# A quantised feed-forward at the end of a two-layer decoder: transposes by DMA, the down projection one tile behind, and a written order for five engines

## The chip, the cores and the metric

The program runs on one core of a Trainium2 chip. A core has a matrix engine (TensorE, here PE, with its weight loads PEld), a vector engine (VectorE, DVE), an activation engine (ScalarE, ACT), a general engine (GpSimd, POOL) and a queue engine that issues DMAs (SyncE, SP). The engines run side by side, each through its own instructions in a fixed order, and wait for each other by semaphores. The metric is the device time of one execution in microseconds (us), as the median over runs.

## The reference, cut to what matters

The model is a decoder of two layers on four batches of 512 rows with 512 features. Each layer has self-attention, cross-attention and a feed-forward, and a layernorm follows every one. The change concerns the last of the six blocks, the second layer's feed-forward, whose weights are rounded to -1, 0 or 1 and whose rows are rounded to 8 bits:

```python
def _quant_act(x):
    s = jnp.max(jnp.abs(x), axis=-1, keepdims=True) / 127.0 + EPS
    xq = jnp.clip(jnp.round(x / s), -128.0, 127.0)
    return (xq, s)

def _qlinear(x, w):
    wq, ws = _quant_weight(w)
    xq, xs = _quant_act(x)
    y = jnp.einsum('bsi,oi->bso', xq, wq)
    return y * xs * ws

gate = jax.nn.silu(_qlinear(x, w_gate))
up = _qlinear(x, w_up)
return _qlinear(gate * up, w_down)
...
x = _layernorm(x + _L1_ffn_ref(x, L1_ffn_w_gate, L1_ffn_w_up, L1_ffn_w_down), axis=-1)
```

Gate and up go from 512 to 2048 features, down goes back to 512. A row's scale needs its largest absolute value, so the down projection of a row can begin only when all of its 2048 hidden values are there.

## The kernel before, in words

All 2048 rows stay in SBUF as 16 tiles `X[t]` of 128 rows by 512 features in float32. The blocks follow one another; the weights of the last feed-forward are loaded, scaled and rounded to bfloat16 during the block before it, the cross-attention (`quantized`).

That cross-attention (`l1_xattn`, its loop in `run`) runs under a manual schedule: a loop over steps writes down the order of the instructions on PE, DVE and ACT by hand. Each step computes scores twice (`first_pass`, L1214, for the row maxima of L1218; `second_pass`, L1230, for the exponentials of L1234), and other work is hung on certain steps with `plan(step, place, function)`. POOL and SP aren't in that schedule; a scheduler orders their instructions. The last batch's output projection (L1287, added in at L1292) ends the block.

The feed-forward (`l1_ffn`, L1419 to L1482) has no written order: the scheduler arranges all engines. It goes over the 16 tiles with `pipelined`, which calls `first` for tile t+1 before `second` for tile t.

`first(t)` rounds the rows (`quantize`: maximum L1426, scale L1427 and L1429, division on DVE L1430, narrowing to bfloat16 on ACT L1431). The rounding is done by adding and subtracting the large constant `ROUND`. A matmul needs its left operand with the features along the partitions, so `flipped` turns the tile: four PE transposes of 128x128 (L1437) into PSUM and one DVE copy out of it (L1438). For each of four parts of 512 hidden features, PE then sums four matmuls for gate (`ps_s`) and four for up (`ps_m`); these go through the helper `mm`, so they carry line L160. ACT applies silu with the row's scale (L1455), DVE multiplies by up and its scale (L1456).

`second(t)` takes the largest absolute value of the 2048 hidden values (L1462, L1463), the scale (L1464, L1465), divides (four of L1468 on DVE), narrows (four of L1469 on ACT), turns 16 blocks on PE with four copies on DVE (L1437, L1438), sums 16 down matmuls in `ps_m` (L160), and adds the scaled sum to `X[t]` (L1476). After the fourth tile of a batch, `layernorm` computes moments (L219, L220), a square root on ACT (L243, with a table load, since silu's table is another), a reciprocal (L244), four norms on DVE (L239), and stores the four tiles (L1480).

PSUM has three banks for `ps_s`, two for `ps_t`, three for `ps_m` in this block.

Of the kernel before, what the change touches and what calls it, by code (L numbers as in the profile page):

```python
# [10 lines left out]
BF16 = mybir.dt.bfloat16  # L11
# [6 lines left out]
P = 128  # L18
B, S, F = 4, 512, 512
T = B * S  # L20
# [66 lines left out]
def decoder_kernel(ctx: ExitStack, tc: tile.TileContext, a: dict, out: bass.AP):  # L87
# [134 lines left out]
    def inverse_roots(b):  # L222


        mv, y = moments[b]
        v, t = small(4, "var"), small(4, "newton")
        G.tensor_scalar(v, mv.rearrange("p (t s) -> p t s", s=2)[:, :, 1], LN_EPS, None, ALU.add)
# [8 lines left out]
    def normalise_tile(b, i):  # L236
        mv, rstd = moments[b]
        x = X[4 * b + i]
        V.tensor_scalar(x, x, mv[:, 2 * i:2 * i + 1], rstd[:, i:i + 1], ALU.subtract, ALU.mult)  # L239

    def table_roots(b):
        mv, rstd = moments[b]
        A.activation(rstd, mv.rearrange("p (t s) -> p t s", s=2)[:, :, 1], AF.Sqrt, bias=LN_EPS)  # L243
        V.reciprocal(rstd, rstd)  # L244
# [864 lines left out]


# [6 lines left out]
    def l1_xattn():  # L1117
# [189 lines left out]
        for M in range(4 * B):  # L1307
# [40 lines left out]
            for i in range(4):  # L1348
                plan(t0 + norms[i], LATE, normalise_tile, b, i)
        for name, n, steps in (("L1_ffn_gateT", INNER, (2, 17, 19)), ("L1_ffn_upT", INNER, (35, 53, 54)),  # L1350
                               ("L1_ffn_downT", F, (68, 85, 110))):
            quantized(plan, name, n, *steps)
# [66 lines left out]
    def l1_ffn():  # L1419
# [4 lines left out]
        def quantize(x, scratch, xq, s):  # L1424

            V.tensor_reduce(s, x, AX.X, ALU.max, apply_absolute_value=True)  # L1426
            V.tensor_scalar(s, s, 1.0 / 127.0, Q_EPS, ALU.mult, ALU.add)  # L1427
            inv = small(1, "one", 8)
            V.reciprocal(inv, s)  # L1429
            V.tensor_scalar(scratch, x, inv, ROUND, ALU.mult, ALU.add)  # L1430
            A.activation(xq, scratch, AF.Copy, bias=-ROUND)  # L1431

        def flipped(dst, src, n):
            for c in range(n // 4):
                pt = pst(BF16)
                for i in range(4):
                    PE.transpose(pt[:, tk(i)], src[:, tk(4 * c + i)], identb)  # L1437
                V.tensor_copy(dst[:, 4 * c:4 * c + 4, :], pt.rearrange("p (k n) -> p k n", k=4))  # L1438

        def first(t):  # L1440
            s = small(1, "one", 8)
            xq, xqt = tmp(BF16), prob("q", [4, P], 3, BF16)
            quantize(X[t], tmp(), xq, s)
            flipped(xqt, xq, 4)
            gs, us = small(1, "one", 8), small(1, "one", 8)
            V.tensor_tensor(gs, s, sg, ALU.mult)
            V.tensor_tensor(us, s, su, ALU.mult)
            h = [prob("P", [512], 8) for _ in range(4)]
            for n in range(4):
                pg, pu = pss(), psm()  # L1450
                nn = slice(512 * n, 512 * n + 512)
                mm(pg, chunks(xqt), [w[:, nn] for w in wg])
                mm(pu, chunks(xqt), [w[:, nn] for w in wu])
                g = tmp()
                A.activation(g, pg, AF.Silu, scale=gs)  # L1455
                V.scalar_tensor_tensor(h[n], pu, us, g, ALU.mult, ALU.mult)  # L1456
            return h

        def second(t, h):
            part, s, inv = small(4, "part4"), small(1, "one", 8), small(1, "one", 8)  # L1460
            for n in range(4):
                V.tensor_reduce(part[:, n:n + 1], h[n], AX.X, ALU.max, apply_absolute_value=True)  # L1462
            V.tensor_reduce(s, part, AX.X, ALU.max)  # L1463
            V.tensor_scalar(s, s, 1.0 / 127.0, Q_EPS, ALU.mult, ALU.add)  # L1464
            V.reciprocal(inv, s)  # L1465
# [70 lines left out]
```

## Time and profile before

| What | us |
|---|---|
| median of three runs | 2851.83 |
| the three runs | 2848.3 to 2853.07 |
| the profiled execution's own time | 2832.23 |
| its span | 2830.5 |
| first gate matmul of the last feed-forward, from the span's start | 2611.22 |
| last addition of a down sum begins | 2821.31 |

The span is the time from the first to the last recorded instruction of one profiled execution. For each engine the page gives busy time and instructions; a second view gives the same by stage, with the granted PE clock as a share of full speed. Another follows the chain of work that ended last: start, length, engine, tile and line of each piece, each released by the one before it. A line of the timeline has start, length, engine, line, operation, the tile written and those read with their shapes, how often, and in brackets how long the engine had been idle and for whom. A line on DMAs has the tiles, the issuing queue, the number, the size and the median time from issue to landing. PE's matmuls are pipelined and their ends are modelled, so the distance from one group's start to the next is the better measure of them.

### The profile page before, as it was taken

To read this page: it belongs to the slowest core of one execution; us is meant where nothing else is said; L and a number is where in the kernel's file an instruction comes from. 1 tells how busy PE (TensorE), PEld (TensorE's weight loads), DVE (VectorE), ACT (ScalarE), POOL (GpSimd) and SP (SyncE) were. 2 spreads that over 40 slices of the span, in tenths; PEclk is the share of its full clock that TensorE was granted. 3 is DMA by queue.
4 is the path that set the end of the run, shared out by engine and by line. 5 is a ranking of instruction groups with operands and counts; after the bars stand their busy time and mean duration, and the time that the engine had idled before them with its cause. 6 is when DMAs were issued, how large, how long until landed. Compare 5 with 4: busy or idle time off the path is not lost.

```text
span 2830.5 us, 30402 instructions
## 1 busy us (share of the span) xinstructions
PE 2714.3 (96%) x11434; PEld 1329.1 (47%) x11434; DVE 1693.2 (60%) x3551; ACT 1050.4 (37%) x1929; POOL 423.0 (15%) x436
## 2 busy tenths in 40 slices
PE   7999999898989989999999999999999999999897
PEld 3444444474556435555555555553334334334443
DVE  4555554554211467566765665665766766675998
ACT  2333433233222123233323332233565564554443
POOL 3000000024000401001101110124332332211000
PEclk9999999899999999999999999999999999999999
DMA  9700000002330301000000000110112021010000
GB/s 391 294 15 1 15 5 27 23 16 94 127 113 21 129 30 60 0 1 1 1 0 1 1 1 30 45 64 34 60 60 71 27 87 45 12 53 1 16 16 31
DMA packets 61128, 142.76 MB, mean 50 GB/s; under 512 B 6537, under 2 KB 26010, under 8 KB 54818
## 3 DMA queue, kind: packets, MB, share of 16 engines
q1 hardware_dynamic: 54818, 123.80, 12.2%
q0 software_dynamic: 6144, 16.79, 1.7%
q8 instruction: 99, 1.62, 0.2%
q14 instruction: 67, 0.55, 0.1%
HBM read 84.73 MB, written 47.45 MB: 47 GB/s over the span
## 4 chain that ended last, share of the span: by engine, by line
PE 57%; DVE 7%; ACT 1%; issue 1%; POOL 0%; DVEq 0%; ACTq 0%; POOLq 0%
PE ps_m L160 16%; PE ps_b L1230 8%; PE ps_m L934 7%; PE ps_m L979 5%; PE ps_s L947 5%; PE ps_m L1241 4%; PE ps_t L964 2%; PE ps_m L1162 2%; PE ps_b L1214 2%; PE ps_m L1287 2%; DVE P L1456 1%; PE ps_m L1176 1%; PE ps_s L160 1%; DVE P L1468 1%; PE ps_m L1223 1%
## 5 line engine op out<-in xcount | busy, mean ns | idle before, releaser
L1218 DVE TENSOR_REDUCE maxes<-ps_b 128x2 f32<-128x1024 f32 x256 | 312.7, 1223 | 178.3 <-PE ps_b L1214 177.9
L160 PE MATMUL ps_m<-w,attnT 128*128 128x512 f32 (+1 forms) x992 | 382.0, 539 | 0.0
L1234 ACT ACTIVATE PT<-ps_b 128x1024 f32<-128x1024 f32 x256 | 260.9, 1023 | 234.6 <-PE ps_b L1214 152.2
L1214 PE MATMUL ps_b<-k,q 32*128 32x512 f32 x1024 | 286.3, 640 | 1.7 <-ACT PT L1234 1.6
L1230 PE MATMUL ps_b<-q,k 32*128 32x512 f32 x1024 | 283.6, 639 | 0.6 <-ACT PT L1234 0.6
L934 PE MATMUL ps_m<-xT,w 128*128 128x512 f32 x512 | 261.1, 595 | 0.0
L313 DVE TENSOR_TENSOR x<-x,ps_m 128x512 f32<-128x512 f32 x128 | 88.0, 687 | 264.0 <-PE ps_m L160 263.8
L160 PEld LDWEIGHTS ps_m<-w,attnT 128*128 128x128 f32 x736 | 139.0, 191 | 168.6 <-issue 163.8
L951 ACT ACTIVATE P<-ps_s,nmax 128x512 f32<-128x512 f32 (+3 forms) x256 | 135.2, 528 | 182.1 <-DVE nmax L949 179.7
L906 POOL TENSOR_TENSOR q<-tmp 128x512 f32<-128x512 f32 x64 | 81.2, 1269 | 692.6 <-DVE tmp L905 624.3
L947 PE MATMUL ps_s<-k,q 128*128 128x512 f32 (+3 forms) x512 | 180.1, 434 | 0.9 <-ACT P L951 0.9
L370 ACT ACTIVATE P<-ps_s,nmax 128x512 f32<-128x512 f32 x128 | 88.5, 693 | 203.4 <-DVE nmax L368 203.4
L979 PE MATMUL ps_m<-PT,v 128*128 128x512 f32 (+3 forms) x512 | 161.6, 436 | 1.6 <-ACT PT L969 1.6
L969 ACT COPY PT<-ps_t 128x512 f32<-128x512 f32 (+1 forms) x128 | 61.1, 477 | 239.3 <-PE ps_t L964 239.3
L160 PE MATMUL ps_m<-w,xT 128*128 128x512 f32 (+1 forms) x384 | 143.6, 529 | 3.3 <-DVE v L338 3.3
L1230 PEld LDWEIGHTS ps_b<-q,k 32*128 32x128 f32 x1024 | 75.9, 183 | 147.3 <-issue 119.9
L964 PEld LDWEIGHTS ps_t<-kc,P 128*128 128x128 f32 x640 | 83.8, 141 | 120.9 <-issue 79.2
L1241 PE MATMUL ps_m<-PT,vv 128*32 128x512 f32 x1024 | 136.4, 605 | 0.6 <-ACT PT L1234 0.6
L979 PEld LDWEIGHTS ps_m<-PT,v 128*128 128x128 f32 x512 | 92.3, 192 | 94.3 <-issue 50.4
L348 PE MATMUL ps_m<-xT,w 128*128 128x512 f32 x256 | 121.0, 599 | 10.6 <-DMA w<-in_L_attn_Wq 10.6
L949 DVE TENSOR_REDUCE nmax<-ps_s 128x1 f32<-128x512 f32 (+3 forms) x256 | 124.7, 487 | 4.6
L948 DVE TENSOR_TENSOR ps_s<-ps_s,mask 128x128 f32<-128x128 f32 x256 | 73.1, 289 | 80.3 <-PE ps_s L947 80.3
(285 smaller groups left out, 4439.7 us busy)
## 6 DMA issues: line engine op xcount, KB each, us to landing
hidden<-w SPq DMA_DIRECT2D x16, 1024.0 KB, 17.0
result<-w SPq DMA_DIRECT2D x16, 1024.0 KB, 16.9
w<-in_L_ffn_gateT SPq DMA_DIRECT2D x8, 1024.0 KB, 5.0
tmp<-tmp POOLq DMA_DIRECT2D x64, 128.0 KB, 2.0
w<-in_L_ffn_upT SPq DMA_DIRECT2D x8, 1024.0 KB, 4.9
w<-in_L_ffn_downT SPq DMA_DIRECT2D x8, 1024.0 KB, 5.1
w<-in_L_attn_Wqkv SPq DMA_DIRECT2D x6, 1024.0 KB, 7.0
w<-in_L_attn_Wo SPq DMA_DIRECT2D x5, 1024.0 KB, 12.2
```

What stands on the lines that cost most here:

```text
L160: PE.matmul(ps, lhsT=x, rhs=y, start=(i == 0), stop=(i == n - 1))
L934: PE.matmul(ps_q[n], lhsT=wq[h // 4][:, i, tk(h % 4)], rhs=st["xt"][:, i, :], start=(i == 0), stop=(i == 3))
L947: PE.matmul(s[:, :w], lhsT=q[:, tk(qi)], rhs=k[:, :w], start=True, stop=True)
L949: V.tensor_reduce(nmax[:, qi:qi + 1], s[:, :w], AX.X, ALU.max, negate=True)
L951: A.activation(p[:, :w], s[:, :w], AF.Exp, bias=nmax[:, qi:qi + 1], accum_out=sums[:, qi:qi + 1])
L964: PE.transpose(pt[:, tk(qi)], probs[qi][:, tk(c)], ident)
L979: PE.matmul(av[:, c * P:], lhsT=st["v"][:, c, tk(g)], rhs=pts[c][:, c * P:], start=(c == 0), stop=(c == 3))
L1214: PE.matmul(s[:, j, :], lhsT=q[strip(i), tk(qi)], rhs=k[strip(i), :], start=True, stop=True)
L1218: V.tensor_reduce(at[:, 2 * half:2 * half + 2, 16 * (1 - g % 2)], s, AX.X, ALU.max, negate=True)
L1230: PE.matmul(s[:, j, :], lhsT=k[strip(i), tk(c)], rhs=q[strip(i), :], start=True, stop=True)
L1234: A.activation(p, s, AF.Exp)
L1241: PE.matmul(avs[g][strip(i), :], lhsT=vv[c][:, 4 * m + i, 16 * par:16 * par + 32], rhs=pts[g, c, i // 2][:, i % 2, :], start=(c == 0), sto ...
```

## The change

The rows of tiles 0 and 1 are rounded during the cross-attention, in six pieces planned at its steps 113 to 118 (`first_rows`). In the feed-forward, division of the rows and half of the division of the hidden values go to POOL. All turning is done by DMA transposes issued from SP (`dma_start_transpose`): one of 128x512 for a tile's rows, two of 128x1024 for its hidden values, both in bfloat16, straight from SBUF to SBUF; PE's transposes and DVE's copies go. Maxima, divisions and narrowings of the hidden values work on 1024 features at once. The down matmuls of tile k-1 stand behind the gate and up matmuls of tile k (the last three tiles' down matmuls stand at the end). Moments are computed tile by tile; the root of all but the last two tiles is computed on POOL by Newton steps (`inverse_roots`), the norm is applied on ACT by scale and shift for all but the last, and each tile is stored by itself. The whole loop is under a manual schedule for PE, DVE, ACT, POOL and SP, so the order of the lines is the order of the instructions on each. `inverse_roots`, `normalise_tile` and `table_roots` get parameters for one tile.

The diff, cut:

```diff
-    def normalise_tile(b, i):
+    def normalise_tile(b, i, engine=V):
...
+    def scale_of_row(s):
+        inv = small(1, "one", 8)
+        V.tensor_scalar(s, s, 1.0 / 127.0, Q_EPS, ALU.mult, ALU.add)
+        V.reciprocal(inv, s)
+        return inv
+
+    def largest(t):
+        s = small(1, "one", 8)
+        V.tensor_reduce(s, X[t], AX.X, ALU.max, apply_absolute_value=True)
+        rounded[t] = s, scale_of_row(s)
+
+    def divide(t, x):
+        G.tensor_scalar(x, X[t], rounded[t][1], ROUND, ALU.mult, ALU.add)
+
+    def turn_rounded(t, x, xq, xqt):
+        A.activation(xq, x, AF.Copy, bias=-ROUND)
+        nc.sync.dma_start_transpose(xqt, xq)
+        rounded[t] = rounded[t][0], xqt
...
+        for t in range(2):
+            for part in range(3):
+                plan(113 + 3 * t + part, LATE, first_rows, t, part)
...
-        def quantize(x, scratch, xq, s):
-        def flipped(dst, src, n):
-        def first(t):
-        def second(t, h):
-        pipelined(range(T // P), first, second)
...
+        def scales_of(t):
+            scales[t] = small(4, "sums", 3)[:, 0:2]
+            G.tensor_scalar(scales[t], both, rounded[t][0], None, ALU.mult)
+
+        def gate_and_up(t, n):
+            if n == 0:
+                hidden[t] = [prob("h", [2, 512], 4) for _ in range(2)], small(4, "nmax", 3)[:, 0:2]
+            pg, pu, g = pss(), psm(), prob("silu", [512], 3)
+            nn, xs = slice(512 * n, 512 * n + 512), chunks(rounded[t][1])
+            mm(pg, xs, [w[:, nn] for w in wg])
+            mm(pu, xs, [w[:, nn] for w in wu])
+            A.activation(g, pg, AF.Silu, scale=scales[t][:, 0:1])
+            V.scalar_tensor_tensor(hidden[t][0][n // 2][:, n % 2, :], pu, scales[t][:, 1:2], g,
+                                   ALU.mult, ALU.mult)
+
+        def largest_of(t, i):
+            h, part = hidden[t]
+            V.tensor_reduce(part[:, i:i + 1], flat(h[i]), AX.X, ALU.max, apply_absolute_value=True)
+
+        def divide_hidden(t):
+            h, part = hidden[t]
+            s, ds = small(1, "one", 8), small(1, "one", 8)
             V.tensor_reduce(s, part, AX.X, ALU.max)
+            inv = scale_of_row(s)
+            for i, engine in enumerate((V, G if t < N - 1 else V)):
+                engine.tensor_scalar(flat(h[i]), flat(h[i]), inv, ROUND, ALU.mult, ALU.add)
+            G.tensor_tensor(ds, s, sd, ALU.mult)
+            hidden[t] = h, ds
+
+        def turn_hidden(t, i):
+            hq, hqt = prob("hq", [1024], 3, BF16), prob("hqt", [8, P], 6, BF16)
+            A.activation(hq, flat(hidden[t][0][i]), AF.Copy, bias=-ROUND)
+            nc.sync.dma_start_transpose(hqt, hq)
+            turned.setdefault(t, []).extend(chunks(hqt))
+
+        def down(t):
+            ps_d[t] = pst()
+            mm(ps_d[t], turned.pop(t), wd)
+
+        def add_down(t):
+            V.scalar_tensor_tensor(X[t], ps_d.pop(t), hidden.pop(t)[1], X[t], ALU.mult, ALU.add)
+            tile_moments(t // 4, t % 4)
+            (inverse_roots if t < N - 2 else table_roots)(t // 4, slice(t % 4, t % 4 + 1))
+
+        def store(t):
+            mv, rstd = (x[:, t % 4 * n:] for x, n in zip(moments[t // 4], (2, 1)))
+            if t == N - 1:
+                normalise_tile(t // 4, t % 4)
+            else:
+                shift = small(1, "one", 8)
+                G.tensor_scalar(shift, mv[:, 0:1], rstd[:, 0:1], -1.0, ALU.mult, ALU.mult)
+                A.activation(X[t], X[t], AF.Identity, scale=rstd[:, 0:1], bias=shift)
+            nc.sync.dma_start(out[tk(t), :], X[t])
...
+        with tc.manual_schedule(engines={e.engine for e in engines}):
+            for k in range(N):
+                ahead = k + 2 < N
+                if 2 <= k < N - 1:
+                    add_down(k - 2)
+                if k:
+                    turn_hidden(k - 1, 0)
+                gate_and_up(k, 0)
+                if k:
+                    turn_hidden(k - 1, 1)
+                if ahead:
+                    largest(k + 2)
+                gate_and_up(k, 1)
+                largest_of(k, 0)
+                if ahead:
+                    x = prob("x", [512], 2)
+                    scales_of(k + 2)
+                    divide(k + 2, x)
+                gate_and_up(k, 2)
+                gate_and_up(k, 3)
+                if 2 <= k < N - 1:
+                    store(k - 2)
+                if ahead:
+                    turn_rounded(k + 2, x, prob("xq", [512], 2, BF16), prob("xqt", [4, P], 3, BF16))
+                largest_of(k, 1)
+                divide_hidden(k)
+                if 1 <= k < N - 2:
+                    down(k - 1)
+            for i in range(2):
+                turn_hidden(N - 1, i)
+            for t in (N - 3, N - 2, N - 1):
+                down(t)
+                add_down(t)
+                store(t)
```

In the order that results, the first four gate matmuls of tile 0 stand in PE's order ahead of the last attention group's transposes of its sums (L1261). In SP's order the two first row transposes stand ahead of the last load of the down weights.

## The prediction

> **What bounds the kernel now.** I read four views in this order: the busy shares, the busy time by stage, the chain that ended last over one tile, and the end of the timeline.
>
> The first lines of the page (span; then busy time, share and instructions of each engine):
> ```profile
> span 2830.5 us, 30402 instructions
> PE 2714.3 (96%) x11434; PEld 1329.1 (47%) x11434; DVE 1693.2 (60%) x3551; ACT 1050.4 (37%) x1929; POOL 423.0 (15%) x436
> ```
> PE looks saturated, but the share is a mean over all stages, and the change touches only the last 220 us. Busy time by stage, each stretch two tiles long (PE, PEld, DVE, ACT, POOL; then granted clock, DMA share, GB/s):
> ```profile
> 2635.00:2661.00 26.00, 24.11 (x138) 11.71 (x137) 24.52 (x64) 12.34 (x21) 0.00 (x0) 1.00 0.00 1
> 2661.00:2687.00 26.00, 23.80 (x135) 11.51 (x133) 23.43 (x63) 11.58 (x18) 0.00 (x0) 1.00 0.11 41
> 2687.00:2713.00 26.00, 23.19 (x138) 11.49 (x137) 24.46 (x65) 12.71 (x22) 0.00 (x0) 1.00 0.00 1
> ```
> Here DVE is as busy as PE (24.5 of 26 us), ACT half, POOL idle, DMA near idle. The chain over one tile shows what sets the pace:
> ```profile
> 2646.86 1.04 PE ps_s L160 x4
> 2647.89 0.86 PE ps_m L160 x4
> ...
> 2652.32 0.76 DVE P L1456
> 2653.10 0.69 DVE part L1462
> ...
> 2654.10 0.74 DVE P L1456
> 2654.84 0.66 DVE attnT L1438 x2
> 2655.51 0.59 DVE part L1462
> ...
> 2656.93 0.60 DVE one L1426
> 2657.53 1.19 DVE P L1468 x3
> 2658.71 0.66 DVE x L1476
> 2659.37 0.34 DVE q L1438
> 2659.72 0.05 issue
> 2659.76 0.39 PE ps_s L160
> ```
> Next tile's first gate matmul (2659.76) starts 12.90 us after this one's (2646.86). The first half of the chain is matmuls at 0.86 us for four (0.216 each); the second half is DVE work in a row, ending in L1438, the copy out of PSUM of the rounded rows that PE has turned. So the stage is a loop PE to DVE to PE, with DVE's order in it, and not PE alone. Over the stage: first gate matmul 2611.22, last down sum added from 2821.31; 210.1 us for 16 tiles, 13.13 each (the layernorm at the end of a batch costs some).
>
> The end of the timeline:
> ```profile
> 2821.31 0.75 DVE L1476 SCALAR_TENSOR_TENSOR x<-ps_m,one,x 128x512 f32<-128x512 f32 x1 [2.48 <-PE ps_m L160]
> 2823.49 1.92 DVE L239 TENSOR_SCALAR x<-x,mv,rstd 128x512 f32<-128x512 f32 x4
> 2824.07 1.80 SPq L1480 DMA_DIRECT2D out<-x  x4
> ```
> From the last addition to the end of the span 9.2 us: four norms, four stores.
>
> **The change part by part.** *PE.* The 20 transposes a tile go. What stays is 48 matmuls, 48 x 0.216 = 10.37 us. If nothing else delays PE, 16 tiles take 165.9 us instead of 210.1: **-44.2**.
>
> *Can DVE follow?* It loses five PSUM copies (0.416 each), the norm (0.54), half of the hidden rounding and the row rounding (0.48). Left per tile: four products 4 x 0.748 = 2.99; two maxima over 1024, not shown in this form, between 2 x 0.68 x 2 = 2.72 (L1462 twice) and 2 x 1.22 = 2.45 (L1218, from PSUM), I take 2.45 to 2.72; row maximum 0.68; add-down 0.75; moments 0.69 + 0.18; one division over 1024 0.735 (L1090); five small ones at 0.15. Sum 9.2 to 9.5, under 10.37.
>
> *POOL* gets 15 one-column root instructions (4.7 us from 2583.46 to 2589.26 with the 1.04 us of L1091 taken out), three small ones (0.2 each), a division over 512 and one over 1024. L1091 shows 1.04 for 1024 with constants; with a per-row scalar the bounds are 1.04 and, by L906's 1.27 for 512, 2.5. POOL: 6.9 to 9.1, under 10.37 too. I take the low end, same operation class. *ACT*: four silus 0.685, two narrowings of 1024 at 1.05 (L1096), 0.63 for the row (L1431), about 0.62 for the norm: 6.1. Silu, copy and norm share a table in the changed order, so the eight table loads inside the stage (four L243, four L1455, 1.28 each, at batch ends) shrink to three around its start and one in the tail. *SP* gets four issues a tile, 0.39 each by the store row (L1480), in the order hidden half 0, half 1, store, rows.
>
> *The queue that decides: DMA transposes.* Per tile two of 256 KB and one of 128 KB, all in SP's queue. The trace has none. Rows, KB and us from issue to landing:
> ```profile
> tmp<-tmp POOLq DMA_DIRECT2D x64, 128.0 KB, 2.0
> result<-P SPq DMA_DIRECT2D x18, 256.0 KB, 2.2
> w<-turned SPq DMA_DIRECT2D x32, 64.0 KB, 3.9
> bias<-in_b_rows SPq DMA_DIRECT2D x5, 256.0 KB, 8.4
> ```
> Bounds for 256 KB: 2.2 (plain copy) and 8.4. I take 4.0, of which 2.0 hold the queue: the nearest in kind is the 64 KB row that is spread over few partitions (3.9), since a turn, too, breaks rows up. Then a tile's queue is busy 2.0 + 2.0 + 1.0 = 5.0 of 10.37 us.
> On the deadline: in the steady loop hidden(t) is divided about 10.5 us after its tile's first matmul (last matmul 6.9, product 0.75, maximum 1.2, small ones 0.6, division 0.74, handovers). ACT narrows half 0 first thing in the next tile: 11.7, half 1 behind one silu: 13.4. PE wants half 0 at 10.37 + 6.91 = 17.3 and half 1 eight matmuls later, 19.0. So a landing may take 5.5 us before PE waits; 4.0 fits. Behind the two narrowings stand the silus: silu 0 runs at 12.3 instead of 11.4, but PE has three banks for gate and three for up (5.2 us of lead), so PE doesn't feel it.
>
> The Trainium skill speaks both ways here. *VectorE: DVE Perf Modes*, "The three transpose paths", gives the DMA crossbar 1309 ns for 128x128 in bf16 against 390 ns on TensorE; taken one block after another that would be 20 x 1.31 = 26 us a tile, an estimate of some 250 us lost. *DMA: Bandwidth & Descriptors*, "Latency and other measured facts", has 261 GB/s for a DMA transpose; 640 KB a tile would then be 2.5 us, an estimate with no loss. Neither is shown by a run here, and neither is a term of the sum.
>
> *Head.* First rows of tiles 0 and 1 are rounded and turned during the cross-attention, at its steps 113 to 118. DVE's share of it, 2 x (0.68 + 0.30), lies beside a PE that is the bound there (in the last 97 us of that stage DVE waited 19.3 us for score matmuls, PE 4.8 for anything): 0, at most +2. In exchange the four transposes, their copy and PE's 0.72 wait between 2609.9 and 2611.22 go, -1.3, and the first four gate matmuls now stand in PE's order where it waited 0.94 for DVE's sums, **-2.2** in all.
> *Filling the pipe.* In tile 1 no down matmuls lie between: its first silu waits behind tile 0's narrowing, which comes 4.7 us after tile 0's last matmul plus the old batch's four norms (0.42 each at pace); PE runs out of gate banks for about 1.6 us, and down(0) then waits some 2.1 for its turned half: **+3.7**.
> *Tail.* Behind the last up matmul PE has two held-back down groups, 6.9 us. With no down group between tiles 14 and 15 ACT is late as in tile 1: its last silu ends some 2.5 after the last up matmul. Then product 0.75, maximum 1.2, small ones 0.6, division 0.74, narrowing 1.05 and 4.0 of landing: 10.8, less 6.9, so PE stands about **+4.0**. From the last addition on only one tile is normed and stored: three norms of 0.48 less, **-1.6**.
>
> Sum: -44.2 - 2.2 + 3.7 + 4.0 - 1.6 = -40.3, and +0.5 for the mixing in the cross-attention: **-40**. The profiled execution took 2832.23 (span 2830.5) and would take 2792; the runs' median, 2851.83, is 19.6 us higher for a cause the trace doesn't show, so I carry the difference over: **2812**.
>
> **The rivals.** *Late turns, still a gain.* If a 256 KB turn holds the queue 4.6 us, a tile takes 2.5 x 4.6 = 11.5 instead of 10.37: 16 x 1.13 = 18, so 2830. For it: nothing here shows a turn. Against: every 256 KB row that isn't queued behind others is below 3.
> *Orders that catch on each other.* Five engines now have a written order. If DVE works 15% slower beside POOL (9.5 becomes 10.9) with a handover or two, 11.3 a tile: +15, 2827. Against: L1090 takes 0.72 to 0.75 beside POOL's L1091.
> *Slower than before: the turns are the bound.* Place: SP's queue, three turns a tile. It decides from 10.37 + 40/16 = 12.87 us a tile, which is 12.87/2.5 = 5.15 us of queue for 256 KB. At 6 us a tile takes 15.0: 16 x 4.63 = +74, 2812 + 74 = 2886. For it: the 8.4 us row, if it is time of moving and not of queueing. Against: it fell in the start, with DMA busy 97%.
> *No effect:* that the new order leaves DVE the pace-setter at about 13: then near 2850. Against: its sum of 9.5.
>
> **How the numbers follow.** Forecast 0.60 (own range 2803 to 2822: landing 2.3 to 5, and the runs' own spread of some 5 us); late turns 0.16; catching orders 0.08; turns as the bound 0.13; no effect 0.03. Within 0.2% (6 us), what a measurement can hardly tell from no change, lies only the last. Faster 0.84, same 0.03, slower 0.13. The range leaves out the bound turns and the worst of the late ones: 2802 to 2845.
>
> **What will show it.** Right: in the last stage gate matmuls 10.4 us apart, tile to tile; PE's busy time near the stretch; waits of PE only in tile 1 and before the last down group; turns landing within 5.5 us; DVE near 9.5 of 10.4. Wrong: PE waiting for hqt at every down group (turns late), SP's queue without gaps (turns the bound), or gate matmuls waiting for silu (orders catch). The prediction falls if a 256 KB turn holds the queue above 4 us, or if the first 2590 us change by more than 2 us.

## The result: 2815.18 us against 2852.09, and the profile after

The median of four runs of the changed kernel is 2815.18 us (2806.61 to 2818.3), that of the kernel before 2852.09 (2848.3 to 2853.07). The ratio is 0.9868 with a 95% interval of 0.9848 to 0.9888, so 37 us faster. The prediction had 2812, faster. The sum behind it was less good than its result, and most of what follows is about that.

The page of the changed kernel begins as follows (span; then busy time, share and instructions of each engine):
```profile
span 2816.5 us, 29952 instructions
...
PE 2700.2 (96%) x11097; PEld 1313.9 (47%) x11114; DVE 1642.5 (58%) x3313; ACT 1047.2 (37%) x1905; POOL 511.9 (18%) x724
```
The shares say as little as before: 14 us less of PE and 51 us less of DVE don't show what happened. The view by stage does, again with stretches of two tiles (PE, PEld, DVE, ACT, POOL; then granted clock, DMA share, GB/s):
```profile
2651.12:2671.84 20.72, 20.61 (x96) 9.37 (x97) 18.77 (x37) 11.61 (x16) 12.35 (x41) 1.00 0.38 86
2671.84:2692.55 20.71, 20.61 (x95) 9.40 (x96) 17.91 (x33) 11.76 (x16) 11.95 (x41) 1.00 0.41 92
2692.55:2713.30 20.75, 20.64 (x96) 9.43 (x97) 17.95 (x33) 11.76 (x16) 12.00 (x41) 1.00 0.48 90
```
Two tiles take 20.7 us instead of 26 or so, PE is busy in all of it, DVE in 17.9 to 18.8 of it, POOL in 12, and the DMA engines some 40% of it. The chain over one tile has nothing but PE in it:
```profile
2672.00 0.86 PE ps_s L160 x4
2672.86 0.86 PE ps_m L160 x4
...
2678.91 3.45 PE ps_t L160 x16
2682.36 0.86 PE ps_s L160 x4
```
From one tile's first gate matmul to the next it is 10.36 us. The loop from PE to DVE and back, which set the pace before, is gone.

The end of the timeline, and the last drains (an engine's closing instruction at the end of the program, line L1609: how many, duration in ns as minimum, median and maximum, first and last start):
```profile
2799.73 1.46 PE L160 MATMUL ps_t<-w,hqt 128*128 128x512 bf16 x3 [3.09 <-DMA hqt<-hq]
...
2804.86 0.26 POOL L1524 TENSOR_SCALAR one<-mv,rstd 128x1 f32<-128x1 f32 x1 [2.66 <-DVE rstd L244]
2805.14 0.75 DVE L1514 SCALAR_TENSOR_TENSOR x<-ps_t,one,x 128x512 f32<-128x512 f32 x1 [0.38 <-POOL one L1524]
```
```profile
L1609 POOLq DRAIN  x3: 44/113/10873, 2804.8 to 2816.2; - x3
L1609 SPq DRAIN  x3: 7/7/13, 2810.4 to 2815.9; - x3
```
PE stands 3.09 us for the last tile's turned rows. From the last addition (2805.14) to the end of the span it is 11.4 us, where it was 9.2 before and 7.6 were predicted. POOL's drain begins at 2804.8, as POOL's last instruction, the shift of tile 14, comes up, and takes 10.9 us. SP, which has the stores, is done at 2810.4 and waits for it.

**A measure for what follows.** The profiled spans differ by 14 us only (2830.5 and 2816.5), the medians by 37. The stage alone is a firmer measure: from the last matmul of the cross-attention's output projection (its last start is 2609.9 before, 2631.4 after) to the end of the span. It is 2830.5 - 2609.9 = **220.6 us before and 185.1 after**, 35.5 less. (In the changed kernel the four gate matmuls that moved ahead, 0.9 us, lie in front of this mark.) Where the other 20 us lie, before the stage, the third experiment tells. "Stage" below means this measure.

### The profile page after: what moved, and what is told of

Same layout as the page of the kernel before. It is cut to its first block, busy times and chain, and to the rows that moved or that the text cites. A ratio compares the mean times of both kernels' runs of the same rounds, so it can differ in the third digit from the quotient of the medians.

```text
span 2816.5 us, 29952 instructions
## 1 busy us (share of the span) xinstructions
PE 2700.2 (96%) x11097; PEld 1313.9 (47%) x11114; DVE 1642.5 (58%) x3313; ACT 1047.2 (37%) x1905; POOL 511.9 (18%) x724
## 4 chain that ended last, share of the span: by engine, by line
PE 59%; DVE 4%; issue 1%; ACT 1%; another core or an unknown queue 1%; POOL 0%; DVEq 0%; POOLq 0%; ACTq 0%
PE ps_m L160 16%; PE ps_b L1255 8%; PE ps_m L934 7%; PE ps_m L979 5%; PE ps_s L947 5%; PE ps_m L1266 4%; PE ps_t L964 2%; PE ps_m L1187 2%; PE ps_b L1239 2%; PE ps_m L1312 2%; PE ps_s L160 2%; PE ps_t L160 1%; PE ps_m L1201 1%; DVE maxes L1243 1%
## 5 line engine op out<-in xcount | busy, mean ns | idle before, releaser
L160 PE MATMUL ps_m<-w,attnT 128*128 128x512 f32 x736 | 324.0, 598 | 9.8 <-DVE x L313 9.8
L947 PE MATMUL ps_s<-k,q 128*128 128x512 f32 (+3 forms) x512 | 180.1, 434 | 0.8 <-ACT P L951 0.8
L160 PE MATMUL ps_m<-w,xT 128*128 128x512 f32 (+2 forms) x414 | 151.8, 519 | 4.0 <-DVE v L338 3.4
L160 PE MATMUL ps_m<-PT,w 128*128 128x512 f32 (+1 forms) x248 | 115.5, 594 | 7.7 <-PEq L833 3.8
```

What stands on the lines that cost most here:

```text
L160: PE.matmul(ps, lhsT=x, rhs=y, start=(i == 0), stop=(i == n - 1))
L947: PE.matmul(s[:, :w], lhsT=q[:, tk(qi)], rhs=k[:, :w], start=True, stop=True)
```

## The experiments

All ratios are to the kernel before, from runs on the same chip as the experiment's.

**1. The tail without GpSimd.** Tiles 13 to 15 take the root from the table and the norm on DVE, and the last hidden scale is multiplied on DVE.
```diff
-            G.tensor_tensor(ds, s, sd, ALU.mult)
+            (G if t < N - 1 else V).tensor_tensor(ds, s, sd, ALU.mult)
...
-            (inverse_roots if t < N - 2 else table_roots)(t // 4, slice(t % 4, t % 4 + 1))
+            (inverse_roots if t < N - 3 else table_roots)(t // 4, slice(t % 4, t % 4 + 1))
...
-            if t == N - 1:
+            if t >= N - 3:
                 normalise_tile(t // 4, t % 4)
```


> In the tail GpSimd gets nothing: tiles 13 to 15 take their roots from the table and their norm on VectorE, and the last hidden scale is multiplied on VectorE. GpSimd's last instruction is then the scale of tile 14 (2787.1 in the changed kernel's profile) instead of the shift of tile 14 (2804.9). Theory 1 (GpSimd's drain sets the end): its 10.8 us begin near 2787 after the span's start of the changed kernel, end near 2798, and lie beside work; from the last addition to the end of the span 6 to 7 us instead of 11.4, so the kernel gains 4.5 to 5.5 us over the changed one. Theory 2 (the end of a program takes about 8.5 us after the last store is issued, whatever GpSimd did): the drain is still the last thing, the end moves by less than 1 us.

Measured: median 2807.21, ratio 0.9853 (0.9836 to 0.9869), stage 180.1, so 5.0 less than the changed kernel; from the last addition (2793.19) to the end of the span 6.5 us. Its drains:
```profile
L1609 POOLq DRAIN  x3: 44/174/12318, 2773.7 to 2799.4; - x3
L1609 SPq DRAIN  x3: 7/7/13, 2798.4 to 2799.0; - x3
```
POOL's drain now starts at 2773.7, as its last division begins, and is over at 2786, beside PE's work; SP's at 2798.4 is the last. Theory 1 holds: the drain's place, not its being there, cost 5 us.

**2. The changed kernel once more.** No edit.

> The changed kernel once more, for comparison on the same chip. The feed-forward's part (first gate matmul behind the cross-attention to the last addition) repeats the first profile's within 1 us: tiles 10.37 us apart, a wait of about 3.1 us before the last down group, 10.8 us of drain on GpSimd from 2 us before the last addition. Theory 1 on the 20 us that the profile of before lacks against its own runs: the gather of the layer-0 feed-forward (925 to 990 us) is the only stage that differs by more than 2 us between profiles, and differs from execution to execution. Theory 2: it is a property of the changed program (its code lies elsewhere), then it repeats within 2 us in every execution.

Measured: median 2815.83, ratio 0.9879 (0.9862 to 0.9895); span 2816.7, stage 185.0, tiles 10.36 apart, wait before the last down group 3.17, drain of 10,872 ns from 2805.0. The stage repeats within 0.1 us. The first matmul of layer 1's attention starts at 990.6 here and at 990.0 in the first profile, so this run alone would have spoken for theory 2, a property of the program. The other experiments, whose program is the same there, speak against it: they start that attention at 978.7 (experiment 1), the others between 979.9 and 988.0; and the changed kernel's own four runs spread over 11.7 us (2806.61 to 2818.3).

**3. The kernel before once more.** No edit.

> The kernel before, profiled once more. Theory 1 (its first profile caught a lucky gather in the layer-0 feed-forward, which its timed runs did not have): the first matmul of layer 1's attention starts 976 to 992 us after the span's start, not at 970.5, and from there to the end it takes 1859 to 1861 us as before: span 2836 to 2852. Theory 2 (the 20 us between the first profile and the timed runs lie elsewhere, or come with timing as such): the gather's stage repeats within 2 us of 970.5.

Measured: 2853.75, span 2852.0, first matmul of layer 1's attention at 991.0 instead of 970.5; from there to the end 1861.0 us (before: 1860.0), stage 220.6 again. The stretch in front of it is the gather of layer 0's feed-forward. The waits there (window from 900 to 1000; us in total, times, longest; `remote` means that this profile doesn't show who ended the wait), once in this profile of the kernel before, once in the changed kernel's:
```profile
DVE x L313 <- remote: 22.4, 4, 9.1
```
```profile
DVE x L313 <- remote: 15.4, 2, 9.1
```
The first profile of the kernel before has no such line. So one kernel shows both, 970.5 and 991.0; the first profile had caught a short gather. The 19.6 us between it and its runs' median, which the prediction carried over as unexplained, are this. Why the gather takes 0 to 20 us longer in most executions is open.

**4. First rows not planned into the cross-attention.** Rounding and turning of tiles 0 and 1 are written at the head of the feed-forward, outside the manual schedule.
```diff
+        late = rounded.setdefault("late", [])
...
-                plan(113 + 3 * t + part, LATE, first_rows, t, part)
+                late.append((first_rows, t, part))
...
+        for f, t, part in rounded.pop("late"):
+            f(t, part)
         for t in range(2):
             scales_of(t)
```


> The first rows of tiles 0 and 1 are rounded and turned when the feed-forward begins, not during the cross-attention. Theory 1 (the head was a gain of 2.2): PE then stands for a row maximum 0.68, scale 0.3, division 0.7, narrowing 0.6 and a landing of 3.2, in all 5.5 us, less the 2 us by which the layer's last additions are ready ahead of PE's last matmul: 4 to 6 us longer than the changed kernel. Theory 2 (the rows were hidden by other work anyway, or their place in the cross-attention costs what it saves): within 1 us.

Measured: median 2816.14, ratio 0.9888 (0.9868 to 0.9907), stage 185.2, as the changed kernel. But the edit didn't make the rows late: in its trace the first maximum of L1121 starts at 2264.6, where the changed kernel has it at 2553.2. Outside the written order the scheduler moved the rows ahead, as their tile is finished early. The run only shows that this work fits in anywhere; what late rows cost wasn't measured.

**5. Norm and all of the hidden division on DVE again.**
```diff
-            for i, engine in enumerate((V, G if t < N - 1 else V)):
+            for i, engine in enumerate((V, V)):
...
-            if t == N - 1:
+            if True:
                 normalise_tile(t // 4, t % 4)
```


> The second half of the hidden division and the norm go back from GpSimd and ScalarE to VectorE. VectorE is busy 8.98 us a tile in the changed kernel; with a division of 0.75 and a norm of 0.5 it needs 10.2 of the 10.37 that PE takes. Theory 1 (PE alone paces the stage): the pitch stays between 10.37 and 10.7, the stage 0 to 5 us longer. Theory 2 (VectorE was the pace-setter and these two moves are what freed it): the pitch goes to 11 or more, from 0.6 x 16 = 10 us up. In both, GpSimd's last work lies earlier only by the shifts.

Measured: median 2810.1, ratio 0.9865 (0.9848 to 0.9883), stage 182.0: not slower than the changed kernel but 3.1 us faster. By stage (columns as above):
```profile
2654.71:2675.43 20.72, 20.61 (x96) 9.39 (x97) 20.03 (x39) 10.32 (x14) 8.26 (x36) 1.00 0.42 95
```
DVE is busy 20.03 of 20.72 us and PE still doesn't wait for it: PE paces, theory 1, and the two moves to ScalarE and GpSimd bring nothing as things stand. The 3 us come from the drain again: without the shifts POOL's last work lies earlier, its drain of 10.8 us starts 3.4 us ahead of the last addition (2795.1 and 2798.53) instead of 0.3, and the end follows (8.2 us from the last addition instead of 11.4).

**6. Turning on PE again, in the changed kernel's order.** Narrowing stays where it is; the transposes of the first half stand behind the second group of gate and up matmuls of the next tile, those of the second half behind the third, those of the next rows ahead of the down group.
```diff
-            nc.sync.dma_start_transpose(hqt, hq)
-            turned.setdefault(t, []).extend(chunks(hqt))
+            pending[t, i] = hqt, hq
...
+        def flipped(dst, src, n):
+            for c in range(n // 4):
+                pt = pst(BF16)
+                for j in range(4):
+                    PE.transpose(pt[:, tk(j)], src[:, tk(4 * c + j)], identb)
+                V.tensor_copy(dst[:, 4 * c:4 * c + 4, :], pt.rearrange("p (k n) -> p k n", k=4))
...
                 gate_and_up(k, 1)
+                if k:
+                    flip_hidden(k - 1, 0)
...
                 gate_and_up(k, 2)
+                if k:
+                    flip_hidden(k - 1, 1)
```


> The changed kernel's order, with the turning back on TensorE and its copies on VectorE. Theory 1 (as predicted: the transposes' time on PE and the copies on VectorE are what the gain is): PE needs 48 x 0.216 + 5 x 0.39 = 12.3 us a tile, VectorE 8.98 + 5 x 0.37 = 10.8, so tiles come 12.3 to 12.8 us apart and the stage is 30 to 38 us longer than in the changed kernel: most of the 44 us is gone again. Theory 2 (the written order and the shift of work to other engines are the gain, the turning lay in PE's gaps): the pitch stays under 11.2, less than 13 us longer.

Measured: median 2840.36, ratio 0.9973 (0.9957 to 0.999), stage 214.2: 29 us longer than the changed kernel, 6.3 shorter than before. A piece of its timeline:
```profile
2674.75 0.61 PE L1512 MATMUL ps_t<-identb,hq 128*128 128x128 bf16 x8
...
2677.14 3.62 PE L160 MATMUL ps_t<-w,hqt 128*128 128x512 bf16 x16
2681.10 1.04 PE L160 MATMUL ps_s<-w,xqt 128*128 128x512 bf16 x4 [0.34 <-DVE xqt L1513]
```
Tiles come 11.98 us apart: 10.37, then 1.1 for the transposes (0.45 from the start of eight to the next group, twice, and 0.22 for four), and 0.5 around the wait for the copy of the rows. Theory 1 in kind, though 11.98 lies under its 12.3 to 12.8 and 29 under its 30 to 38: in a stream of matmuls four transposes cost 0.22, not the 0.39 that I had taken. Of the 29 us, 19.5 are this pace from tile 2 to tile 14, 3.1 lie before tile 2, and 11.7 between tile 14's first gate matmul and the last addition (waits of 3.8 for tile 15's rows and 5.8 in the last down groups among them); 5.1 less lie behind the last addition, where POOL's drain is covered.

**7. Turning by DMA alone, in the kernel before.**
```diff
-            for c in range(n // 4):
-                pt = pst(BF16)
-                for i in range(4):
-                    PE.transpose(pt[:, tk(i)], src[:, tk(4 * c + i)], identb)
-                V.tensor_copy(dst[:, 4 * c:4 * c + 4, :], pt.rearrange("p (k n) -> p k n", k=4))
+            for c in range(0, n, 8):
+                w = min(8, n)
+                nc.sync.dma_start_transpose(dst[:, c:c + w, :], src[:, c * P:(c + w) * P])
```


> The kernel before with one edit: rows and hidden are turned by DMA instead of TensorE and VectorE's copies; order, divisions, norms and down groups as before. Theory 1 (the turns by DMA do it alone): VectorE keeps 12.0 - 5 x 0.37 = 10.2 us a tile, PE 10.4, and the other tile's gate and up matmuls cover narrowing and landing, so 10.6 to 11.5 us a tile, 26 to 40 us faster than before. Theory 2 (the down groups a tile behind are needed as well): hidden rows are ready 10.5 us after the tile's first matmul on VectorE's loop, then 1.05 + 3.2 us of narrowing and landing, which the old order leaves open in part: 12.3 to 13.2 us a tile, 0 to 13 us faster.

Measured: median 2823.45, ratio 0.9901 (0.9877 to 0.9924), stage 195.9: 24.7 of the 35.5 us with this edit alone. Four tiles take 43.8 us, 10.95 each (columns as above):
```profile
2694.00:2737.81 43.81, 42.13 (x193) 18.40 (x193) 42.16 (x106) 24.48 (x39) 0.00 (x0) 1.00 0.40 85
```
PE and DVE are both busy over 96% here; PE's wait in these four tiles is 1.63 us, once, for the turned rows. That is theory 1, though 24.7 lies a little under its 26 to 40: the turns by DMA are the main part. The written order and the other moves bring 6.3 without them (experiment 6) and 35.5 - 24.7 = 10.8 on top of them.

**8 and 9. More turns.** Ahead of each turn of a hidden half, two (then four) more of the same into spare buffers.
```diff
+            for _ in range(2):
+                nc.sync.dma_start_transpose(prob("spare", [8, P], 3, BF16), hq)
             nc.sync.dma_start_transpose(hqt, hq)
```


> Ahead of each turn of a hidden half two more of the same are issued into spare buffers. SyncE's queue then holds 7 turns a tile. Theory 1 (a turn holds the queue 1.23 us, whatever its size): 8.6 us a tile, under PE's 10.37; the second half's turn lands 2.0 us behind PE's wish, every other tile (a wait moves the next wish), so 0.5 to 1.2 us a tile, 8 to 19 us longer than the changed kernel. Theory 2 (turns hold the queue 2.0 us, as predicted): 14 us a tile, 58 us longer. Theory 3 (the queue only issues, the moving is what counts and has room): nothing changes by more than 2 us.

> Ahead of each turn of a hidden half four more of the same are issued: 11 turns a tile. Theory 1 (1.23 us of queue each): 13.5 us a tile, the queue without gaps is the bound, 45 to 58 us longer than the changed kernel, and so slower than before, as the rival of the slower side had it, from a price of the turns that the real ones miss by 5 times. Theory 2 (2.0 us each): 22 us a tile, 185 us longer. Theory 3 (only issuing, moving has room): under 10 us longer.

Measured, one execution each. With two more: 2839.97, stage 210.1, 25 us longer than the changed kernel; the distances from tile to tile alternate (11.13, 13.33, 11.38, 13.21, ...), mean 11.93. With four more: 2905.87, stage 276.1, 91 longer, and 55.5 longer than before; tiles 16.0 us apart on average. The queue of SP with four more:
```profile
2704.49 5.38 SPq L1507 DMA_TRANSPOSE spare<-hq  x4
2709.91 1.33 SPq L1508 DMA_TRANSPOSE hqt<-hq  x1
2711.35 5.39 SPq L1507 DMA_TRANSPOSE spare<-hq  x4
2716.79 1.33 SPq L1508 DMA_TRANSPOSE hqt<-hq  x1
2718.16 0.58 SPq L1528 DMA_DIRECT2D out<-x  x1
2718.84 1.23 SPq L1131 DMA_TRANSPOSE xqt<-xq  x1
2720.18 5.37 SPq L1507 DMA_TRANSPOSE spare<-hq  x4
```
and the same tile by stage (DMA share is the last but one):
```profile
2704.49:2720.18 15.69, 11.93 (x49) 4.98 (x48) 9.05 (x16) 6.08 (x8) 5.98 (x20) 0.91 0.98 193
```
The queue has no gap, and the DMA engines are busy 98%. So the turns can be the bound, and then the kernel is slower than before, as that rival had it. In direction theory 1 holds in both runs, with the alternation that it named, and both of its ranges (8 to 19 and 45 to 58) were too low. With four more, five turns back to back take 6.86 us from issue to issue, 1.37 each and not 1.23, a store holds the queue 0.58, and a tile takes 15.7, not 13.5. With two more the queue still has gaps, and the 25 us are PE's waits for turned hidden rows (25.3 us in 17 waits). Theory 2 (58 and 185) and theory 3 (nothing) fall.

**10. A last down group with PE kept at work.** On top of experiment 1.
```diff
             for t in (N - 3, N - 2, N - 1):
+                if t == N - 1:
+                    for _ in range(3):
+                        mm(pss(), chunks(rounded[t][1]), [w[:, 0:512] for w in wg])
                 down(t)
```


> The kernel with the tail off GpSimd, and three idle groups of four gate matmuls (12, 2.6 us) in PE's order ahead of the last down group, where PE stands 3.1 us for the turned rows; nothing reads what they write. What matters is the last down group: it took 5.3 us from its first matmul in the changed kernel and 5.1 with the tail off GpSimd, at a granted clock of 0.50 to 0.58 over its first 3.4 us, where 16 x 0.216 = 3.5 would do. Theory 1 (standing idle about 3 us costs PE half its clock for the 3.4 us that follow): without the idle time the clock stays at 1.00, the last group takes 3.5 us and the end of the span comes 1.5 to 1.8 us earlier, counted from the cross-attention's last out-projection. Theory 2 (the group is slow because its weights have only just landed by DMA, or by the stores' traffic): it takes 5 us again, nothing gained.

What it was meant to explain, in the changed kernel (columns as above; the stretch of PE's wait, the 3.4 us behind it, then the next):
```profile
2796.53:2799.73 3.20, 0.11 (x2) 0.01 (x1) 2.56 (x6) 0.87 (x1) 1.43 (x8) 1.00 0.65 126
2799.73:2803.13 3.40, 3.18 (x8) 1.19 (x10) 0.00 (x0) 0.87 (x2) 1.79 (x9) 0.50 0.19 36
2803.13:2805.13 2.00, 1.90 (x9) 0.70 (x7) 0.16 (x1) 1.43 (x2) 0.26 (x1) 0.99 0.35 131
```
And measured, with the idle groups in the wait (these, then the 3.4 us behind the landing; timeline below):
```profile
2785.51:2788.50 2.99, 2.70 (x12) 1.08 (x11) 1.64 (x5) 2.42 (x3) 0.00 (x0) 1.00 0.59 115
2788.79:2792.19 3.40, 3.40 (x16) 1.48 (x16) 2.19 (x5) 0.20 (x1) 0.00 (x0) 1.00 0.41 112
```
```profile
2788.78 3.13 PEld L160 LDWEIGHTS <-hqt 128*128 128x128 bf16 x16 [1.01 <-DMA hqt<-hq]
2788.79 3.63 PE L160 MATMUL ps_t<-w,hqt 128*128 128x512 bf16 x16 [0.52 <-DVE x L239]
```
The second bracket names DVE, but the weight load of the same group waited for the rows: their last turn is issued at 2785.52 and the group starts 3.27 us later, where it was 3.25 in the changed kernel. Stage 178.4, 1.6 less than in experiment 1; median 2807.52, ratio 0.9862 (0.9846 to 0.9879), where executions differ by more than this. The clock stays at 1.00 and the group takes 3.6 us instead of 5.2. Theory 1: PE lost half its clock for having stood idle, and matmuls whose results nobody reads keep it.

The Trainium skill has the rule: *TensorE: Matmul & The Clock Gate*, "Why this matters for your kernels", tells to leave no idle gap above about 3 us between bursts of matmuls, since one idle window of the activity monitor halves the clock. The traces here agree in kind: the wait of 3.09 us was followed by a granted clock of 0.50, and the 1.49 and 0.80 while the pipe filled were followed by 1.00. They put the length lower. In the last stage of all fourteen profiles PE stood 2.58 to 6.47 us in 29 places, and the clock of the next 3.4 us was 0.50 to 0.67 behind every one of them, down to the 2.58 (clock 0.53) of experiment 9; behind every wait of 1.92 us or less it was 1.00. Between these it went both ways: 0.65 behind one of 2.13 (experiment 8), 1.00 behind another of 2.13 there and behind one of 2.51 (experiment 6).

**11. The last tile turned on PE.** On top of experiment 1: PE, which stands idle there, turns the last tile's hidden rows, DVE copies them, and the norms of tiles 13 and 14 come last.
```diff
+        def turn_last(i):
+            hq, hqt = prob("hq", [1024], 3, BF16), prob("hqt", [8, P], 6, BF16)
+            A.activation(hq, flat(hidden[N - 1][0][i]), AF.Copy, bias=-ROUND)
+            for c in range(2):
+                pt = psm(BF16)
+                for j in range(4):
+                    PE.transpose(pt[:, tk(j)], hq[:, tk(4 * c + j)], identb)
+                V.tensor_copy(hqt[:, 4 * c:4 * c + 4, :], pt.rearrange("p (k n) -> p k n", k=4))
+            turned.setdefault(N - 1, []).extend(chunks(hqt))
...
+            table_roots(3, slice(1, 3))
+            add_last(N - 1)
```


> The kernel with the tail off GpSimd, and the last tile's hidden rows turned by TensorE, which stands idle there, and copied by VectorE (four copies of about 0.4 us), not turned by DMA; the norms of tiles 13 and 14 come behind the last one. Narrowing ends 1.05 us after the division for the first half, the transposes take 0.5, a copy 0.4; the second half lies 1 us behind. Theory 1 (landing of 3.2 us and the half clock behind the wait are what the tail costs): PE stands under 1 us, the last down group starts 1.7 us earlier and takes 3.5 us instead of 5.1, the two late norms give 0.5 back: 2.5 to 3.5 us faster than with the tail off GpSimd, some 7 to 8 faster than the changed kernel. Theory 2 (VectorE's copies and additions now set the tail): the last addition waits for VectorE, gain under 1.5 us.

Measured: stage 178.2, 1.8 less than experiment 1; median 2805.49, ratio 0.9854 (0.9838 to 0.9871). PE's part went as theory 1 said: it stands 0.3 us ahead of each half's transposes, and the group runs at full clock. The end did not:
```profile
2790.45 3.40 PE L160 MATMUL ps_s<-w,hqt 128*128 128x512 bf16 x15
...
2794.42 0.17 DVE L244 RECIPROCAL rstd<-rstd 128x2 f32<-128x2 f32 x1 [0.27 <-ACT rstd L243]
2794.51 0.73 DVE L1524 SCALAR_TENSOR_TENSOR x<-ps_s,one,x 128x512 f32<-128x512 f32 x1
...
2796.65 1.46 DVE L239 TENSOR_SCALAR x<-x,mv,rstd 128x512 f32<-128x512 f32 x3
```
The down sums are there at 2793.85, the addition stands in DVE's order behind a reciprocal that waits for ACT's root, and three norms follow. So theory 2 has a share in it, and theory 1's range of 2.5 to 3.5 was missed.

**12. DVE's way cleared.** As 11, with the second half copied out of PSUM by ACT, the norms of tiles 13 and 14 on ACT with shifts from DVE, and the last tile's norm right behind its root.
```diff
-                V.tensor_copy(hqt[:, 4 * c:4 * c + 4, :], pt.rearrange("p (k n) -> p k n", k=4))
+                half = hqt[:, 4 * c:4 * c + 4, :], pt.rearrange("p (k n) -> p k n", k=4)
+                if i == 0:
+                    V.tensor_copy(*half)
+                else:
+                    A.activation(*half, AF.Copy)
...
+                V.tensor_scalar(shift, mv[:, 2 * i:2 * i + 1], rstd[:, i:i + 1], -1.0, ALU.mult, ALU.mult)
+                A.activation(X[t], X[t], AF.Identity, scale=rstd[:, i:i + 1], bias=shift)
```


> The kernel with the last tile turned on TensorE, with VectorE's way cleared: ScalarE copies the second half out of PSUM, norms tiles 13 and 14, and VectorE does nothing between the last down group and its addition. Counted from the last matmul of the cross-attention's out-projection to the end of the span: changed kernel 185.1 us, tail off GpSimd 180.1, with the idle groups 178.4, last tile turned on TensorE 178.2. Theory 1 (in the last of these VectorE's order, a reciprocal in the way and two norms behind, costs the rest): 176.3 to 177.2. Theory 2 (ScalarE's copies, table load and norms now set the tail): 178 or more.

Measured: stage 176.4, theory 1; last addition at 2798.27, 6.1 us before the end of the span. Median of five 2802.14 against 2848.73, ratio 0.9836 (0.9823 to 0.985): the lowest median here, and 8.7 us less of stage than the changed kernel. The ratio's interval overlaps those of experiments 1, 10 and 11, so it is the stage that tells them apart.

The stages side by side:

| kernel | stage, us | tile to tile, us | last addition to end, us |
|---|---|---|---|
| before (two profiles) | 220.6, 220.6 | 13.1 | 9.2 |
| changed (two profiles) | 185.1, 185.0 | 10.36 | 11.4, 11.6 |
| turning on PE in the new order | 214.2 | 11.98 | 6.3 |
| turning by DMA in the old order | 195.9 | 10.95 | 8.3 |
| norm and division on DVE | 182.0 | 10.37 | 8.2 |
| tail off GpSimd | 180.1 | 10.36 | 6.5 |
| ... and the last tile on PE, DVE's way cleared | 176.4 | 10.36 | 6.1 |

## Why the prediction was right, and where it was wrong

**Right: the bound and its term.** "48 x 0.216 = 10.37" a tile was the whole pace once the transposes were gone; measured 10.36, and so -44.2 for the tiles. That DVE, POOL, ACT and SP's queue all stay below it was right too: DVE 8.98 a tile (predicted 9.2 to 9.5), POOL 6.0 (6.9 to 9.1), ACT 5.9 (6.1). Experiments 6 and 7 show that the turning is what carried it: the turns by DMA bring 24.7 us alone and 29 on top of the rest, the order and the other moves 6.3 alone and 10.8 on top of the turns.

**Right in direction, off in size: the turns.** The changed kernel's rows (first the DMA table, with the median us from issue to landing; then the turns' line, with durations in ns, and its landings):
```profile
hqt<-hq SPq DMA_TRANSPOSE x32, 3.2
```
```profile
L1506 SPq DMA_TRANSPOSE hqt<-hq x32: 1231/1232/1272, 2644.4 to 2797.8; - x32
...
DMA to landing us min/median/max: 3.0/3.2/4.7
```
I had taken 4.0 for the landing and 2.0 for the queue; it was 3.2 and 1.23 (medians), and 1.23 for the rows of half the size too. With 3 x 1.23 = 3.7 us of queue in 10.36 there was room: with three times the hidden halves' turns the stage is still 10.5 us shorter than before (experiment 8), with five times it is longer, and the rival of the bound turns has its case (experiment 9). The landing lay within the bounds given (2.2 and 8.4). For the queue the prediction had only limits above which a rival begins (4.6 and 5.15 us a turn); 1.23 is far below them.

**Wrong: the end, by 3.8 us.** "From the last addition on only one tile is normed and stored: three norms of 0.48 less, -1.6." It became 2.2 longer. The step counted the norms on DVE and left out what the moves gave POOL to do so late: the root of tile 13 and the shifts of tiles 13 and 14, with the last of which its drain of 10.9 us starts. The drain stood in the profile of before (whose last line is L1524), unseen because it began at 2589.0 and had 240 us of cover:
```profile
L1524 POOLq DRAIN  x3: 44/113/10793, 2589.0 to 2830.2; - x3
```
I had asked where each engine's work lies beside PE's, but not where it ends. Experiments 1 and 5 move its end, and the kernel's end follows.

**Mis-sized: the tail, by 1.5.** Predicted +4.0 of standing; PE stood 3.1 (landing 3.2 instead of 4.0) with 0.4 of smaller waits, but the group behind it took 5.3 us for 3.5. Measured from the first gate matmul of tile 14 to the last addition it is 29.7, 5.5 above 13.8 us of gate and up and 10.4 of down groups. The cost of this wait was not its length alone: experiment 10 gets 1.6 back while PE waits for the same rows.

**Mis-sized: filling and head.** Filling the pipe was predicted at +3.7 and took 2.4: from the first matmul of the feed-forward behind the mark (2632.32, less 0.9 for the four gate matmuls done earlier) to tile 2's first (2651.12) it is 19.7 us, where the matmuls alone take 17.3. PE's two waits, predicted at 1.6 and 2.1, were 1.49 and 0.80; the second ended 3.3 us behind the issue of its turn (2644.37), where a landing of 4.0 had been taken. The head was to bring 2.2, at +0.5 of mixing in the cross-attention. Transposes and copy did go and the four matmuls did move ahead, but PE then stood 0.51 for a bank that DVE's last attention addition (L1317) still held, and the cross-attention became 0.6 longer, four matmuls included. Together 0.6 gained instead of 1.7.

The sum from the cross-attention on is then -44.2 + 2.4 + 5.5 + 2.2 - 0.6 = -34.7 (the spans from its first score matmul, 900.56 and 865.75, give -34.8), where -39.8 was predicted: 5 us short, of which the end has 3.8. The number 2812 came out 3 us below the median because the step that carried the 19.6 us over was right: they belong to layer 0's gather and not to this stage, and experiment 3 shows them in the kernel before. That step was taken without its cause, and the closeness is luck in part: the medians differ by 36.9 where the part that changed gives 34.8, and the changed kernel's four runs alone lie 11.7 apart.

The prediction also said that it falls "if the first 2590 us change by more than 2 us". In the two first profiles they changed by some 20. That condition was badly put: it took a single execution as fixed, and the kernel before alone moves by 20.5 from one profile to the next.

The other rivals: no turn came late in the steady loop, no orders caught on each other (between tiles 2 and 14 PE has no wait above 0.05 us), and "no effect" would have needed DVE to pace; with the norm and the division back on it, it is busy 20.03 of 20.72 us and still doesn't.

On the rules weighed in the prediction: *VectorE: DVE Perf Modes*, "The three transpose paths", read block by block would have made 20 blocks a tile the bound, and no run here shows that, as three instructions a tile held the queue 1.23 us each. *DMA: Bandwidth & Descriptors*, "Latency and other measured facts", has 261 GB/s; with the DMA engines 98% busy in experiment 9, where turns are 11 of 12 issues, it was 193, and for this case the measured figure counts.

## What to carry to other kernels

When work is moved to an engine that was idle, look not only at whether it fits into the pace but at when the engine finishes for good: here a closing of 10.55 us followed the end of GpSimd's last instruction, so its last work must lie at least that long before the end. When PE is the bound, price a wait of 2.6 us or more with the matmuls of the next 3.4 us at about half speed, and fill it if it can't be shortened. Compare a changed stage from a mark inside the trace to the end, since another stage of the same program can move by 20 us between executions of one kernel.

## What the runs showed of the hardware that I had not expected

- GpSimd's drain at the end of the program was over 10.55 us after the end of POOL's last instruction in all fourteen profiles, whether that was a step of a root, a shift or a scale. Its own record is longer, as it begins while the last instructions are still to run: 10.79 to 10.88 us in ten profiles, and 12.32 in the four (experiments 1, 10, 11, 12) where a division and a scale were still to come.
- A DMA transpose within SBUF held SP's queue 1.23 us for 128x512 as for 128x1024 in bfloat16 when it was alone; back to back 1.37 from issue to issue for 128x1024, with the DMA engines 98% busy.
- After a wait of 3.04 to 3.17 us at the end PE's granted clock was 0.50 to 0.58 over the 3.4 us behind it, and in other runs a wait of 2.58 us was enough; with matmuls in the wait it stayed at 1.00.
- Times on other engines that were not on the path: a division of 1024 values on POOL by a scalar of each row took 1.68 us (predicted 1.04, bound 2.5), the norm of 512 on ACT with scale and shift by row 0.81 (predicted 0.62).
- The first steps of layer 1 start 970.5 to 991.0 us into the span in these profiles. The waits lie in layer 0's gather; the cause is open.
